# Summing the paths of a grouped convolution two steps of pairs later, with more buffers for the pairs and fewer for the results

## The chip, the cores and the metric

The kernel runs on one core of a Trainium2 chip. The metric is the device time of one execution in microseconds. TensorE (PE) multiplies matrices into PSUM, VectorE (DVE) and ScalarE (ACT) work elementwise and empty PSUM, GpSimd (POOL) does small elementwise work here and issues the indirect DMAs, and SyncE (SP) issues the plain DMAs.

## The reference

The input is `x`, 8 images of 56 x 56 positions with 256 channels. Layer 0 is a block with 32 parallel paths, layer 1 is attention followed by a mixture of experts:

```python
# layer 0: 32 paths, each 256 -> 4 -> (3x3) 4 -> 256 channels
h = relu(bn(einsum('nhwc,cd->nhwd', x, w1) + b1))
h = relu(bn(conv3x3(h, w2) + b2))
h = relu(bn(einsum('nhwd,dc->nhwc', h, w3) + b3))
x = relu(h.sum(over the 32 paths) + x)
# layer 1: t = the positions as tokens, 8 heads of 32 channels
t = t + attention(layernorm(t))   # q (layernorm(k)^T layernorm(v)) / N, plus its input
# 8 experts, each token goes to its two best
t = t + moe(layernorm(t))         # out = tokens + sum of weight * (gelu(tokens w1 + b1) w2 + b2)
```

The ReLU of each path comes before the sum over the paths, so each of 32 x 256 channels must be computed and passed through the ReLU before it can be added.

## The kernel before

**Chunks and slots.** The positions of one image (3136) are cut into 7 chunks of 448; 8 images make 56 chunks. The main loop runs over slots `s`. In slot `s` it computes the last convolution of chunk `s` (`conv3_steps`), the first of chunk `s+2`, the second of chunk `s+1`, the end of chunk `s-1` (`end_steps`: ReLU of the sum, transposes, head means, variances, the products k^T v), the attention and routing of the chunk eight slots back, and a number of tiles of the experts (`moe_steps`), of 256 tokens each. From slot 57 on nothing of the convolution is left: the last attention chunks and the remaining expert tiles form a tail.

**The order.** TensorE, ScalarE and VectorE execute in program order; the program order within a slot is made by `issue`. Each group of work gets a stretch of the slot, such as 0.12 to 1.0 for `end_steps`; each of its steps has a weight and is placed in the middle of its share of the stretch; all steps are sorted by these positions. GpSimd's and SyncE's instructions are ordered by the framework.

**Pairs and sums.** `conv3_steps` has 32 pairs per chunk, two to a step, so 16 steps of pairs. A pair (`pair`) is two products of 64 x 448 into two PSUM tiles (L587), each of which holds four paths of 32 channels. ScalarE writes relu(first + bias) into a buffer `r` (L592), and VectorE adds max(second, -bias) to it in place (L595), which completes the ReLU up to a constant that is added later. Four pairs form a unit, so a chunk has eight units. `sum_paths` (L608) multiplies the four buffers `r` of a unit by `gather`, a matrix of zeros and ones, which adds up the four paths and places the results in four column groups of one PSUM bank. Units 0 to 3 accumulate the first 128 channels, units 4 to 7 the other 128; after the last unit of each half VectorE adds `x` and writes `u` (L615). `begin` in `end_steps` applies the ReLU to `u` on ScalarE (L643), and TensorE transposes it (`tu`, L655).

In the kernel before, unit `u` is summed behind the step that starts with pair 4u+4, which is the step after the unit's last pair. The last unit of a chunk is summed in the next slot, behind its first step.

**Other work on the same engines.** In `end_steps`, VectorE sums the heads (`hmean`, L667), GpSimd centers (`norm`, L681), ScalarE squares (`sq`, L690), VectorE prepares the variances (`hsd`, L718), GpSimd takes their power (L719), and VectorE makes the inverse (`hinv`, L727).

**PSUM.** Products take their tiles from a pool `ps_mm` of seven banks, in a ring; the sums have one bank of their own (`ps_sum`).

**Experts.** A tile of the experts loads rows and weights, transposes the rows (`te`, L1245), multiplies (`ph`, L1287, then `py`, L1303 and L1307), and ScalarE writes the scaled result to a buffer `y` (L1311), two halves per tile. GpSimd adds each half to the output rows with an indirect DMA (L1325). These scatters are ordered in blocks: those of the second choice of a group of chunks wait until those of the first choice have landed, and so on.

Of the kernel before, what the change touches and what calls it, by code (L numbers as in the profile page):

```python
# [8 lines left out]
F32 = mybir.dt.float32  # L9
BF16 = mybir.dt.bfloat16  # L10
I32 = mybir.dt.int32
F32R = mybir.dt.float32r
AF = mybir.ActivationFunctionType
ALU = mybir.AluOpType
# [11 lines left out]
def kernel(  # L26
# [24 lines left out]
    nc = tc.nc  # L51
    B, N, C = x.shape
# [3 lines left out]
    E = w1.shape[0]  # L56
    HC = 32
    NH = C // HC
    P = 128
# [15 lines left out]
    const = ctx.enter_context(tc.tile_pool(name="const", bufs=1))  # L75
# [90 lines left out]
    setup = setup_pool.__enter__()  # L166
# [36 lines left out]
    for dx in range(3):  # L203
        for g in range(NG):
            nc.scalar.dma_start(
                out=W2s[32 * dx : 32 * dx + 32, g],
                in_=W2[32 * g : 32 * g + 32].rearrange(
                    "q (dy dx o) -> dx q dy o", dy=3, dx=3
                )[dx],
# [18 lines left out]
    def is_chunk(s):  # L228
        return 0 <= s < S
# [176 lines left out]
    for f in range(NF):  # L406
        tp = ps_mm.tile([P, 512], F32, tag="mm", name=f"tp_sb_{f}")
        nc.tensor.transpose(tp[:, :NP], bias3[:, f * P : (f + 1) * P], ident[:NP, :NP])
        b3T = setup.tile([P, NP], F32, name=f"b3T_{f}")
        nc.scalar.copy(b3T, tp[:, :NP])  # L410
        sub = setup.tile([P, NQ, NPL], F32, name=f"sub_{f}")
        nc.vector.tensor_copy(
            sub, b3T.rearrange("q (a r n) -> q a r n", r=2, n=NPL)[:, :, 1, :]
        )
        nc.vector.tensor_reduce(
            sumb[:, f, :], sub.rearrange("q a n -> q (a n)"), AX.X, ALU.add
        )
    setup_pool.__exit__(None, None, None)

    spill = ctx.enter_context(  # L420
        tc.tile_pool(name="spill", bufs=NCH + 4, space=bass.MemoryType.DRAM)
    )
    parts = ctx.enter_context(tc.tile_pool(name="parts", bufs=7))
    one = ctx.enter_context(tc.tile_pool(name="one", bufs=1))
    attn = ctx.enter_context(tc.tile_pool(name="attn", bufs=2))
    payp = ctx.enter_context(tc.tile_pool(name="payp", bufs=3))
# [3 lines left out]
    work = ctx.enter_context(tc.tile_pool(name="work", bufs=2))  # L430
# [39 lines left out]
    M = 2 * E + 1  # L470
# [12 lines left out]
        tc.dram_tile([E * CAPR, ROW], F32, name=f"regions_{k}") for k in range(2)  # L483
    ]
    Wd = tc.dram_tile([E, P, WROW], F32, name="Wd")

    b2hl = const.tile([P, C], F32R, name="b2hl")
    b2s = const.tile([P, C], F32, name="b2s")
    b2l = const.tile([E, C], F32R, name="b2l")
    nc.gpsimd.memset(b2s, 0.0)  # L490
    nc.sync.dma_start(out=b2s[:E], in_=b2)
    nc.vector.tensor_copy(b2hl, b2s)
    nc.vector.tensor_tensor(b2l, b2s[:E], b2hl[:E].bitcast(F32), ALU.subtract)
    nc.sync.dma_start(out=b2hl[E : 2 * E].bitcast(F32), in_=b2l.bitcast(F32))
    pos_i = const.tile([P, 2], I32, name="pos_i")
    pos = const.tile([P, 2], F32, name="pos")
    nc.gpsimd.iota(pos_i, [[P, 2]], base=0, channel_multiplier=1)
# [39 lines left out]
    for e in range(M):  # L537
        nc.gpsimd.memset(offs[:, e : e + 1], float(0 if e == 2 * E else e % E * CAPR + TR))
        nc.gpsimd.memset(code[:, e : e + 1], float(E - e % E))

    below = const.tile([P, M, M], F32, name="below")
    nc.gpsimd.memset(below, 1.0)
    nc.gpsimd.affine_select(
        out=below, in_=below, compare_op=ALU.is_ge, fill=0.0, base=-1,
# [8 lines left out]
        out=earlier, in_=earlier, compare_op=ALU.is_ge, fill=0.0, base=-1,  # L553
# [23 lines left out]
    def pair(s, step):  # L577


        cg, ab, c4 = step // 16 * 4 + step % 4, step // 4 % NQ, step % 4  # L580
        hl = h2s[s]
        tiles = [
            ps_mm.tile([P, 512], F32, tag="mm", name=f"c3_{s}_{step}_{g}") for g in range(2)
        ]
        for g in range(2):
            rows = slice(64 * g, 64 * g + 64)
            product = nc.tensor.matmul(  # L587
                tiles[g][:, :CH], W3hl[rows, ab, cg, :], hl[rows, ab, :], start=True, stop=True
            )
        pace[:] = [product.ins]  # L590
        r = parts.tile([P, CH], F32, tag="r", name=f"r_{s}_{step}")
        nc.scalar.activation(  # L592
            r, tiles[0][:, :CH], AF.Relu, bias=b3t[:, cg, 2 * ab : 2 * ab + 1]
        )
        nc.vector.scalar_tensor_tensor(  # L595
            r, tiles[1][:, :CH], nb3[:, cg, 2 * ab + 1 : 2 * ab + 2], r,
            op0=ALU.max, op1=ALU.add,
        )
        unit[s, step] = r

    def sum_paths(s, u):

        f, ab = divmod(u, NQ)
        if ab == 0:
            sums[s, f] = ps_sum.tile([P, 512], F32, tag="su", name=f"su_{s}_{f}")
        ps = sums[s, f]
        for c4 in range(4):
            nc.tensor.matmul(  # L608
                ps[32 * c4 : 32 * c4 + 32, :CH], gather, unit.pop((s, 4 * u + c4)),
                start=(ab == 0), stop=(ab == NQ - 1),  # L610
            )
        if ab == NQ - 1:
            if f == 0:
                usum[s] = one.tile([P, NF, CH], F32, tag="u", name=f"u_{s}")
            nc.vector.scalar_tensor_tensor(  # L615
                usum[s][:, f, :], sums.pop((s, f))[:, :CH], sumb[:, f, :], xTs[s][:, f, :],
                op0=ALU.add, op1=ALU.add,
            )

    def conv3_steps(s):  # L620
        steps = []
        units = NF * NQ
        for step in range(0, 4 * units, 2):
            if is_chunk(s):
                steps.append((0.7, lambda step=step: (pair(s, step), pair(s, step + 1))))
            if step == 0 and is_chunk(s - 1):
                steps.append((0.9, lambda: sum_paths(s - 1, units - 1)))
            if step and step % 4 == 0 and is_chunk(s):
                steps.append((0.9, lambda step=step: sum_paths(s, step // 4 - 1)))
        return steps  # L630

# [561 lines left out]
    got, weights_of, turned, hidden, ready = {}, {}, {}, {}, []  # L1193
# [73 lines left out]
    def bank_of(i, h, name):  # L1267

        if h == 0:
            n = 1 if apart else 2  # L1270
            v = ps_mm.tile([P, n, 256], F32, tag="mm", name=f"{name}_{i}")
            hidden[i, name] = v
        elif apart:
            v = ps_mm.tile([P, 1, 256], F32, tag="mm", name=f"{name}_{i}_{h}")
        else:
            v = hidden[i, name]
        return v[:, h % v.shape[1], :]
# [17 lines left out]
    def tile_out(i, h):  # L1295
        w = weights_of[i]
        eT, g, _ = turned[i]
        if h == 0:
            hidden[i].append(work.tile([P, 2, C], F32, tag="y", name=f"y_{i}", bufs=4))
        hT, y = hidden[i]  # L1300
        own = slot_of[i][1]
        ps = bank_of(i, h, "py")
        nc.tensor.matmul(  # L1303
            ps, own.to_broadcast([P, P]), b2hl, start=True, stop=False
        )
        for f in range(NF):
            nc.tensor.matmul(  # L1307
                ps, hT[:, f, h * P : (h + 1) * P], w[:, (NF + f) * C : (NF + f + 1) * C],
                start=False, stop=(f == NF - 1),
            )  # L1310
        nc.scalar.activation(y[:, h, :], ps, AF.Identity, scale=g[:, h : h + 1])  # L1311
        ready.append((i, h))
# [32 lines left out]
    def moe_steps(first, last):  # L1345


        steps = []

        def some(fn, i, *args):  # L1350
            if 0 <= i < N_ALL:
                fn(i, *args)

        for n in range(first, last):
            steps.append((0.5, lambda n=n: (some(tile_in, n), tile_add())))
            steps.append((1.0, lambda n=n: (some(tile_mid, n - 1, 0), tile_add())))
            steps.append((1.0, lambda n=n: (some(tile_mid, n - 1, 1), some(take_rows, n + 2))))
            steps.append((1.0, lambda n=n: (some(tile_out, n - 2, 0), some(take_weights, n + 1))))
            steps.append((1.0, lambda n=n: some(tile_out, n - 2, 1)))
        return steps  # L1360
# [34 lines left out]
    for s in range(S + A + 1):  # L1395
        a = s - A
        work_of = []
        if s <= S:
            work_of.append((0.0, 1.0 if is_chunk(s) else 0.1, conv3_steps(s)))
# [104 lines left out]
```

## Time and profile before

| | |
|---|---|
| time, median of 3 runs | 3379.75 us (3368.15 to 3382.17) |
| profiled execution | 3374.9 us, granted TensorE clock 0.951 |
| slots 0 to 7, from first pair to first pair | 37.5 to 40.3 us |
| slots 8 to 15 | 42.5 to 60.4 us |
| slots 16 to 54 | 41.6 to 71.1 us, median 51 us |
| last sum of paths | 2820 us |
| tail after it | 555 us |
| `r` on VectorE, L595 | 1792 of 676 ns |
| `r` on ScalarE, L592 | 1792 of 636 ns |
| sums on TensorE, L608 | 3584 records, 574.5 us busy |
| scatter-add issue on GpSimd, L1325 | 420 of 1578 ns |

How to read it: the busy shares of the engines are averages over stages that differ, the main stage with the convolution and the tail with the experts alone, so the stages have to be looked at one by one. TensorE's records show when a product was issued; a product that waits for its operand is issued late, and the others of the same sum lie before it. The time that TensorE stands between two records of one sum is counted neither as idle time before the sum nor as a long record, unless the records no longer touch.

### The profile page before, as it was taken

How to read it: one execution, taken by the hardware profiler on the slowest of the kernel's cores; microseconds unless marked ns; L12 is line 12 of the kernel's file. 1: busy time of each engine (PE TensorE's matmuls, PEld its weight loads, DVE VectorE, ACT ScalarE, POOL GpSimd, SP SyncE). 2: the span in 40 equal slices, each digit the busy share in tenths (PEclk: the TensorE clock that was granted, in tenths of full speed). 3: DMA queues.
4: the chain of work that ended last, by engine and by line, in shares of the span. 5: the costliest groups of instructions: out<-in, count | busy, mean ns of one | idle time of the engine just before them, and what ended most of it. 6: DMA issues, size and time to landing. Idle time of an engine off the chain costs nothing. (4 is left out here: it accounts for less than half of the span.)

```text
span 3374.9 us, 55166 instructions
## 1 busy us (share of the span) xinstructions
PE 3001.6 (89%) x16677; PEld 1697.5 (50%) x16677; DVE 2179.8 (65%) x5762; ACT 1895.8 (56%) x3799; POOL 1928.4 (57%) x1386
## 2 busy tenths in 40 slices
PE   5888888888898999999999999899989987888698
PEld 2343433443444554555545555455444545676577
DVE  3666777777877777776776777776777774333200
ACT  2656555545565666566655666566656654443345
POOL 2222244444556566657565666746656657777677
PEclk7999989989999999999999999999999999988799
DMA  6432334445466676666666667567665756888797
GB/s 146 121 86 84 91 103 123 120 123 150 129 162 159 164 197 168 166 165 174 175 163 163 159 185 187 148 177 187 158 180 152 187 149 159 201 217 218 173 222 178
DMA packets 341481, 537.72 MB, mean 159 GB/s; under 512 B 59952, under 2 KB 251584, under 8 KB 341184
## 3 DMA queue, kind: packets, MB, share of 16 engines
q1 hardware_dynamic: 257088, 429.93, 43.8%
q0 software_dynamic: 81984, 103.45, 16.9%
q8 instruction: 134, 2.20, 0.3%
q14 instruction: 163, 1.34, 0.1%
q10 hardware_dynamic: 2112, 0.81, 0.1%
HBM read 248.01 MB, written 192.55 MB: 131 GB/s over the span
## 5 line engine op out<-in xcount | busy, mean ns | idle before, releaser
L595 DVE SCALAR_TENSOR_TENSOR r<-c,nb,r 128x448 f32<-128x448 f32 x1792 | 1127.3, 676 | 556.7 <-ACT r L592 482.8
L592 ACT ACTIVATE r<-c,b3t 128x448 f32<-128x448 f32 x1792 | 1033.2, 636 | 359.4 <-PE c L587 338.6
L1325 POOL DMA_INDIRECT out_dram<-y,index x420 | 662.8, 1578 | 356.3 <-ACT y L1311 243.7
L587 PE MATMUL c<-hl,W3hl 64*128 64x448 f32 x3584 | 708.4, 428 | 74.4 <-ACT r L592 37.7
L608 PE MATMUL su<-r,gather 128*32 128x448 f32 x3584 | 574.5, 568 | 64.9 <-DVE r L595 38.4
L1031 POOL DMA_INDIRECT regions<-pay,rrowi x448 | 433.1, 967 | 314.1 <-PE c L587 204.2
L587 PEld LDWEIGHTS c<-hl,W3hl 64*128 64x128 f32 x3584 | 341.9, 188 | 505.6 <-issue 227.1
L1287 PE MATMUL ph<-eT,w 128*128 128x256 f32 x1680 | 468.1, 410 | 55.7 <-DMA w<-Wd 23.8
L1307 PE MATMUL py<-w,hT 128*128 128x256 f32 x1680 | 435.6, 384 | 0.0
L1311 ACT ACTIVATE y<-py,g 128x256 f32<-128x256 f32 x420 | 196.7, 475 | 402.1 <-PE py L1307 303.1
L1287 PEld LDWEIGHTS ph<-eT,w 128*128 128x128 f32 x1680 | 306.9, 198 | 196.9 <-issue 101.8
L719 POOL TENSOR_TENSOR hsd<-hsd,half 112x36 f32<-112x36 f32 x56 | 351.7, 6280 | 78.4 <-DVE hsd L718 77.7
L1291 ACT ACTIVATE hT<-ph,w 128x256 f32<-128x256 f32 x420 | 198.1, 477 | 308.5 <-PE ph L1287 165.6
L1307 PEld LDWEIGHTS py<-w,hT 128*128 128x128 f32 x1680 | 293.9, 193 | 28.7
L681 POOL TENSOR_TENSOR norm<-t,hmean 112x512 f32<-112x512 f32 x112 | 120.2, 1130 | 322.1 <-PE c L587 175.0
L870 PE MATMUL at<-tab,tT 128*112 128x272 f32 x896 | 266.1, 421 | 11.9 <-ACT y L1311 6.8
L608 PEld LDWEIGHTS su<-r,gather 128*32 128x32 f32 x3584 | 104.2, 110 | 272.9 <-issue 135.5
L1303 PE MATMUL py<-b2hl,own 128*128 128x256 f32 x420 | 178.7, 425 | 22.4 <-ACT pay L894 8.1
L870 PEld LDWEIGHTS at<-tab,tT 128*112 128x112 f32 x896 | 149.4, 181 | 92.0 <-issue 17.3
L297 PE MATMUL c<-R,W2t 96*32 96x448 f32 x1344 | 180.1, 567 | 3.9 <-DMA R<-h 3.0
L894 ACT ACTIVATE pay<-X,nm,rs 112x256 f32<-112x256 f32 x224 | 134.9, 603 | 75.1 <-DVE nm L889 64.4
L976 POOL TENSOR_TENSOR rq<-ebase,rq 112x8 f32<-112x8 f32 (+1 forms) x32 | 52.9, 1654 | 197.0 <-DVE rq L975 197.0
(246 smaller groups left out, 3198.5 us busy)
## 6 DMA issues: line engine op xcount, KB each, us to landing
w<-Wd SPq DMA_DIRECT2D x210, 513.0 KB
rows<-regions SPq DMA_DIRECT2D x210, 259.0 KB
xi<-in_x_dram SPq DMA_DIRECT2D x56, 448.0 KB
hl<-hi SPq DMA_DIRECT2D x448, 56.0 KB
tTs<-u SPq DMA_DIRECT2D x56, 448.0 KB
ts<-t SPq DMA_DIRECT2D x56, 448.0 KB
tT<-tTs SPq DMA_DIRECT2D x56, 448.0 KB
X<-ts SPq DMA_DIRECT2D x56, 448.0 KB
```

What stands on the lines that cost most here:

```text
L587: product = nc.tensor.matmul(tiles[g][:, :CH], W3hl[rows, ab, cg, :], hl[rows, ab, :], start=True, stop=True)
L592: nc.scalar.activation(r, tiles[0][:, :CH], AF.Relu, bias=b3t[:, cg, 2 * ab : 2 * ab + 1])
L595: nc.vector.scalar_tensor_tensor(r, tiles[1][:, :CH], nb3[:, cg, 2 * ab + 1 : 2 * ab + 2], r, op0=ALU.max, op1=ALU.add,)
L608: nc.tensor.matmul(ps[32 * c4 : 32 * c4 + 32, :CH], gather, unit.pop((s, 4 * u + c4)), start=(ab == 0), stop=(ab == NQ - 1),)
L719: nc.gpsimd.tensor_tensor(sd, sd, half[:T, :].rearrange("q (k h) -> q k h", k=KT), ALU.pow)
L870: nc.tensor.matmul(ps, tT[:, f, k * T : (k + 1) * T], tables_of[b][:, f, :], start=(f == 0), stop=(f == NF - 1),)
L1031: ins = nc.gpsimd.indirect_dma_start(out=regions[n], out_offset=bass.IndirectOffsetOnAxis(ap=v["row_i"][:, (m - group[0]) * KT + k, n : n ...
L1287: nc.tensor.matmul(ps, w[:, f * C + hf * P : f * C + (hf + 1) * P], eT[:, f, :], start=(f == 0), stop=(f == NF - 1),)
L1291: nc.scalar.activation(hT[:, hf, :], ps, AF.Gelu, bias=w[:, 2 * NF * C + hf : 2 * NF * C + hf + 1])
L1307: nc.tensor.matmul(ps, hT[:, f, h * P : (h + 1) * P], w[:, (NF + f) * C : (NF + f + 1) * C], start=False, stop=(f == NF - 1),)
L1311: nc.scalar.activation(y[:, h, :], ps, AF.Identity, scale=g[:, h : h + 1])
L1325: ins = nc.gpsimd.indirect_dma_start(out=out_rows, out_offset=at, in_=y[:, h, :], in_offset=None, compute_op=ALU.add, **partial,).ins
```

## The change

The sum of a unit moves one more step of pairs back: it comes behind the second step after the unit's last pair. The last unit of a chunk is summed behind the second step of the next slot. In between, eight pairs are in hand where it was six, so the pool of buffers `r` grows from seven to nine. Room for them in SBUF comes from three places: the buffers `y` of the experts' results go from four to three; the two helpers that split the experts' second bias into a high and a low part (`b2s`, `b2l`) move from the permanent pool into the setup pool, whose space is reused; and the mask `below`, which has only zeros and ones, becomes bf16. It is for giving TensorE work between a pair and its sum while ScalarE and VectorE finish the pair.

```diff
+    b2hl = const.tile([P, C], F32R, name="b2hl")
+    b2s = setup.tile([P, C], F32, name="b2s")
+    b2l = setup.tile([E, C], F32R, name="b2l")
...
     setup_pool.__exit__(None, None, None)
...
-    parts = ctx.enter_context(tc.tile_pool(name="parts", bufs=7))
+    parts = ctx.enter_context(tc.tile_pool(name="parts", bufs=9))
...
-    b2hl = const.tile([P, C], F32R, name="b2hl")
-    b2s = const.tile([P, C], F32, name="b2s")
-    b2l = const.tile([E, C], F32R, name="b2l")
...
-    below = const.tile([P, M, M], F32, name="below")
+    below = const.tile([P, M, M], BF16, name="below")
...
         for step in range(0, 4 * units, 2):
             if is_chunk(s):
                 steps.append((0.7, lambda step=step: (pair(s, step), pair(s, step + 1))))
-            if step == 0 and is_chunk(s - 1):
+
+            if step == 2 and is_chunk(s - 1):
                 steps.append((0.9, lambda: sum_paths(s - 1, units - 1)))
-            if step and step % 4 == 0 and is_chunk(s):
+            if step > 4 and step % 4 == 2 and is_chunk(s):
                 steps.append((0.9, lambda step=step: sum_paths(s, step // 4 - 1)))
...
-            hidden[i].append(work.tile([P, 2, C], F32, tag="y", name=f"y_{i}", bufs=4))
+            hidden[i].append(work.tile([P, 2, C], F32, tag="y", name=f"y_{i}", bufs=3))
```

## The prediction

> **What bounds the kernel now.** I read the busy table and the slices first, then stretches of time, then the sums by themselves, then single waits.
>
> ```profile
> PE 3001.6 (89%) x16677; PEld 1697.5 (50%) x16677; DVE 2179.8 (65%) x5762; ACT 1895.8 (56%) x3799; POOL 1928.4 (57%) x1386
> ...
> 85.00:388.00 303.00, 259.29 (x1476) 114.87 (x1468) 207.98 (x407) 177.72 (x321) 71.66 (x35) 0.97 0.34 94
> 388.00:750.00 362.00, 305.22 (x1662) 141.85 (x1662) 275.53 (x684) 195.69 (x380) 168.11 (x116) 0.90 0.39 113
> 750.00:2820.00 2070.00, 1941.10 (x11109) 1035.31 (x11108) 1521.45 (x3911) 1270.35 (x2543) 1255.33 (x850) 0.98 0.64 167
> 2820.00:3375.00 555.00, 449.38 (x2258) 381.31 (x2258) 146.40 (x680) 234.31 (x525) 408.01 (x291) 0.91 0.81 199
> ```
>
> TensorE is the busiest engine everywhere, but least so before 750 us (slots 0 to 15, 85% busy against VectorE's 69 to 76%); up to 2820 us it is at 94%; then comes a tail of 555 us with no conv work. The change acts on the sums (L608), which end at 2820 us.
>
> "Busy" hides something there. A sum is eight records, two for each of its four pairs. Undisturbed, their starts lie within 0.42 us. I read all 448 sums record by record: where a later pair's result is missing, TensorE starts the first records and stands still inside the sum. The excess over 0.42 us adds up to 200 us: 112.5 us in the sums of unit 5 of the chunk, 46.6 in unit 2, 9.1, 6.5, 11.2 and 10.6 in units 1, 3, 4 and 7. Slots 0 to 15 hold 112 us of it, slots 16 to 55 88 us. The timeline of one slot shows why unit 5:
>
> ```profile
> 274.76 6.13 POOL L719 TENSOR_TENSOR hsd<-hsd,half 112x36 f32<-112x36 f32 x1 [6.69 <-DVE hsd L718]
> ...
> 278.97 0.94 PE L608 MATMUL su<-r,gather 128*32 128x448 f32 x4
> ...
> 280.92 0.19 DVE L727 SCALAR_TENSOR_TENSOR hinv<-hsd 112x32 f32<-112x32 f32 x1 [2.32 <-POOL hsd L719]
> ...
> 281.46 2.42 DVE L595 SCALAR_TENSOR_TENSOR r<-c,nb,r 128x448 f32<-128x448 f32 x4
> ...
> 282.16 1.53 PE L608 MATMUL su<-r,gather 128*32 128x448 f32 x4 [2.25 <-DVE r L595]
> ```
>
> VectorE stands at `hinv` until GpSimd's power is ready; the four pair results queued behind it come only then, and TensorE stands with half of a sum issued. Over slots 0 to 55 the list of waits has these two entries:
>
> ```profile
> PEld c L587 <- ACT r L592: 152.0, 281, 3.0
> ...
> DVE hinv L727 <- POOL hsd L719: 67.5, 46, 3.2
> ```
>
> The first is the other limit: the pair products wait for a PSUM bank that ScalarE has not yet emptied.
>
> In the tail, GpSimd's rows show the scatters (L1325) 1.85 us apart, in runs of eight with a gap between:
>
> ```profile
> 3215.09 1.54 POOL L1325 DMA_INDIRECT out_dram<-y,index  x1 [0.30 <-issue]
> 3221.91 1.54 POOL L1325 DMA_INDIRECT out_dram<-y,index  x1 [5.28 <-ACT y L1311]
> 3223.76 1.54 POOL L1325 DMA_INDIRECT out_dram<-y,index  x1 [0.30 <-issue]
> ```
>
> The chain that ended last passes, from 3189 to 3249 us, through the landing of such scatters (4.4 to 6.0 us each) into `ACT y`: four `y` buffers are full there.
>
> **What the Trainium skill says.** "Trainium Architecture — The Big Picture", What this means for kernel authors: engines are independent and one blocks another only through a semaphore. The excerpt agrees: GpSimd's power reaches TensorE only over VectorE, so moving a sum behind other work is what can hide it. "Perfetto Trace Analysis", Matmuls: independent matmul groups should rotate through PSUM banks so that one's evacuation overlaps the next's products. The 152.0 us wait shows that seven banks do this incompletely, and it limits the gain below. [...]
>
> **The change part by part.** Let pN be the step with pairs N and N+1, Su the sum of unit u (pairs 4u to 4u+3). A slot's order comes from positions between 0 and 1, worked out from the weights. Before: p20 .644, S4 .6875, hinv .69, p22 .731, p24 .769, S5 .8125, p26 .856, p28 .894. After: p20 .644, p22 .682, hinv .69, S4 .7255, p24 .769, p26 .807, S5 .8505, p28 .894. So every second pair step comes 4.9% of a slot (some 2.5 of 51 us) earlier against all other work, and sums come 3.8% later.
>
> *Unit 5.* p22 now stands ahead of hinv on VectorE, so S5 no longer needs anything behind that wait. The first instruction that does is p28: pair 28's first product takes the bank seven allocations back, the second product of pair 24, whose result is the first behind hinv, where S5 had needed the second. TensorE gains p26 (0.67 us) and half of S5 (0.5 us) as cover, and the needed result is 0.6 us earlier: up to 1.8 us less standing per slot. Capping each slot's measured excess at 1.8 us leaves 14.0 + 13.9 us in slots 0 to 15 and 41.3 us in 16 to 55.
>
> *Units 1, 3, 4, 7.* Their pairs are two steps old at the sum; the excess goes: 27.5 us in slots 0 to 15, 10.1 after.
>
> *Unit 2.* S2 waits for pair 11 behind VectorE's `hmean` (1.21 us). In the new order p14 stands before S2 and needs the banks of pairs 10 and 11, so it waits for the same result. But p14's evictions now come ahead of ScalarE's `sq`, which waits for GpSimd. Ends nothing and all; I take 40%: 10.6 us early, 8.0 later.
>
> *How much passes to the end.* From slot 16 on TensorE is 94% busy, so I pass on 80%: 0.8 x (41.3 + 10.1 + 8.0) = 47.5 us. Before that ScalarE and VectorE take turns with it: 60%, 0.6 x (27.9 + 27.5 + 10.6) = 39.6 us. Gain 87 us.
>
> *Nine buffers of pairs.* Eight pairs are issued when a sum runs, where it was six with seven buffers; the one spare stays. The write of pair 4u+9 waits for Su, which is ahead of that pair's own products on TensorE, so it hides: 0.
>
> *The slot's start.* S7 of the last chunk moves from .0625 to .1005, ScalarE's `u` (L643) stays at .125, and evictions of p4 and TensorE's turn of `u` are queued behind it. Today `u` starts 2.04 us after S7 ends. New order in slot 5: S7 would end about 1.6 us later (255.5 instead of 253.9), VectorE's `u` (0.68 us) then stands behind pairs 2 and 3 and ends near 256.5, where ScalarE started at 255.98 until now: 0.5 us late, with TensorE waiting at `tu` already. From slot 16 on the attention product (1.17 us, L870) and the router's small VectorE work lie there and hide it. 16 x 0.5 = 8 us; ends 0 and 56 x 1.4 = 78, if nothing hides.
>
> *Three `y` buffers.* I took each tile's `y` start and the start of its second scatter; with landings of 4.4 to 6.0 us, a `y` would find its buffer three tiles back unlanded in 33 to 43 of 210 cases, all after 2870 us, and with four in 3 to 11. Between 3182 and 3250 us GpSimd sets the pace (8 x 1.85 + 5.2 = 20 us for four tiles, 5.0 a tile, against 4.13 a tile of TensorE later): a buffer is back 6.0 + 0.5 us after its last scatter, and the tile three on is due at GpSimd after five more scatters, 9.25 us. Hidden. From 3258 us TensorE sets it, and there the counted delays are 1.9 to 3.5 us once, kept to the end: 3 us, with 1 for the earlier ones, 4 us; ends 0 and 12.
>
> *The rest.* The bias split (0.29 and 0.41 us on VectorE at 64 us) only moves ahead in the setup, and `below` as bf16 is read in 17 instructions of 0.28 to 0.75 us: 0, at most 1 us either way.
>
> Sum: 3380 - 87 + 8 + 4 = 3305 us.
>
> **The rivals.**
>
> - *The wait moves to the banks.* The ring of seven makes a later pair wait for nearly the result the sum had waited for. For it: 152.0 us of bank waits, and S2 as worked out. Against: p22 passes hinv. Only pairs handed on earlier remain, some 20 us, against 12 of costs: 3372 us, no change.
> - *Slower: the later sum 7 and the fewer `y`.* ScalarE stands for VectorE's `u` in every slot and half passes on (39 us), the tail costs 12, the gain is 20: 3411 us. For it: ScalarE is in order and two steps of evictions lie behind `u`. Against: it is 56% busy, and after slot 16 other work fills the place.
> - *A larger gain.* Once TensorE runs ahead, the gaps of VectorE go too (it waits 477.8 us for evictions), and all 200 us of standing go with part of TensorE's 74 us of idle before products: 3380 - 200 + 12 = 3192 at the extreme, 3230 as a middle. Against: GpSimd's power and the banks don't get faster.
>
> **How the numbers follow.** Main case 0.62, larger gain 0.13, banks 0.13, slower 0.12. The prediction is the main case, 3305 us. Its pass-on share and unit 2 move it between 3250 and 3350; the range goes on down to 3240, short of half of the larger gain, and up to 3395, which takes in the banks and part of the slower case. Faster by over 0.5%: 0.62 + 0.13 + a third of the banks' case, 0.79; within: 0.09; slower: 0.12.
>
> **What would show it.** Right: the starts inside S5 lie within 0.42 us in nearly all slots, `hinv` still waits for GpSimd, slots before 750 us get 2 to 3 us shorter and later ones about 1 us, and the tail is some 4 us longer with more `ACT y` waits on scatters. Wrong: TensorE's waits before products (L587) grow by what the sums lose; or ScalarE's `u` waits over a microsecond for VectorE in late slots too; or the tail grows by more than 12 us.

## The result, and the profile after

The changed kernel takes 3495.95 us (median of 4 runs, 3484.67 to 3501.05), the kernel before 3376.24 us in the same runs: 1.0352 times as long, 95% interval 1.0314 to 1.0389. The forecast of 3305 us was wrong in direction, and the time lies outside its range of 3240 to 3395 us.

First the busy table and the same four stretches as before: their bounds, length, then busy time (with instructions) of PE, PEld, DVE, ACT and POOL, granted clock, DMA share and GB/s.

```profile
PE 3044.4 (87%) x16677; PEld 1742.9 (50%) x16677; DVE 2170.5 (62%) x5762; ACT 1906.8 (55%) x3799; POOL 1922.0 (55%) x1386
...
85.00:388.00 303.00, 256.39 (x1422) 110.81 (x1422) 201.62 (x389) 174.03 (x308) 71.64 (x35) 0.91 0.30 87
388.00:758.00 370.00, 310.46 (x1700) 146.53 (x1696) 276.38 (x696) 199.07 (x386) 166.88 (x116) 0.88 0.39 114
758.00:2928.00 2170.00, 1978.33 (x11118) 1078.17 (x11114) 1513.27 (x3909) 1280.03 (x2547) 1247.33 (x850) 0.95 0.61 159
2928.00:3490.00 562.00, 455.91 (x2281) 385.25 (x2279) 149.58 (x686) 236.09 (x528) 410.64 (x293) 0.90 0.80 197
```

From first pair to first pair, slots 0 to 15 take 700.8 us (685.4 before), slots 16 to 55 take 2169.9 (2071.9), the tail 561.8 (557.7). So of the 115 us between the two profiled executions, 98 were lost where the forecast saw a gain of 47. VectorE, ScalarE and GpSimd are busy for the same time as before within 0.6%; what is longer is time in which something waits, and in the third stretch the clock fell from 0.98 to 0.95.

The groups of instructions on TensorE (busy us, mean ns, then idle us before them with the releasers); from the loop of `conv3_steps` on, a line of the changed kernel has a number one higher than before:

```profile
L587 PE MATMUL c<-hl,W3hl 64*128 64x448 f32 x3584 | 780.1, 440 | 134.9 <-ACT r L592 59.2 <-DVE r L595 50.3 <-DMA hl<-lo 9.2
L608 PE MATMUL su<-r,gather 128*32 128x448 f32 x3584 | 448.5, 571 | 4.3 <-DVE u L615 4.3
L748 PE MATMUL kv<-norm 112*128 112x129 f32 x896 | 173.2, 358 | 79.2 <-POOL norm L738 78.8 <-DVE r L595 0.2
L656 PE MATMUL tu<-ident,u 128*112 128x128 f32 x448 | 73.5, 289 | 39.3 <-ACT u L644 39.2
```

The sums did what the change is for: the standing inside them (what the starts of a sum's eight records exceed 0.42 us by, added over all 448 sums) fell from 200.0 to 11.2 us, their busy time from 574.5 to 448.5, the idle time before them from 64.9 to 4.3. But idle time before the products k^T v (`kv`, L747 before) grew from 16.9 to 79.2 us, before the pair products from 74.4 to 134.9, and before `tu` from 18.6 to 39.3. TensorE's records name the releaser, GpSimd's `norm` at L738, which the forecast had not looked at. The list of waits shows the same chain, engine by engine (us in total, times, longest):

```profile
PEld c L587 <- ACT r L592: 231.7, 454, 5.2
POOL hsd L720 <- DVE hsd L719: 146.5, 46, 10.9
DVE kvs L756 <- PE kv L748: 119.4, 47, 8.1
DVE hinv L728 <- POOL hsd L720: 100.2, 49, 7.8
PE kv L748 <- POOL norm L738: 78.8, 73, 4.0
ACT y L1312 <- DMA out_dram<-y,index: 60.7, 19, 10.0
ACT u L644 <- DVE u L615: 50.0, 31, 2.5
PE tu L656 <- ACT u L644: 39.2, 31, 1.8
```

Before, GpSimd's power waited 77.7 us for `hsd`, `kvs` 17.8 for `kv`, `hinv` 75.3, `kv` 1.2 for `norm`, `tu` 8.1 for `u`. The timeline of one slot of the changed kernel shows where the lateness begins; it is put together from the lines of VectorE, GpSimd and TensorE. ScalarE has finished the squares of this chunk at 1575.37 us:

```profile
1576.54 1.28 DVE L595 SCALAR_TENSOR_TENSOR r<-c,nb,r 128x448 f32<-128x448 f32 x2 [2.28 <-ACT r L592]
...
1580.06 1.28 DVE L595 SCALAR_TENSOR_TENSOR r<-c,nb,r 128x448 f32<-128x448 f32 x2 [0.98 <-ACT r L592]
1581.25 1.21 DVE L700 TENSOR_REDUCE hss<-sq 112x32 f32<-112x1024 f32 x1
...
1583.57 0.17 DVE L719 TENSOR_SCALAR hsd<-hss 112x32 f32<-112x32 f32 x1
...
1583.83 6.16 POOL L720 TENSOR_TENSOR hsd<-hsd,half 112x36 f32<-112x36 f32 x1 [2.43 <-DVE hsd L719]
...
1590.02 0.19 DVE L728 SCALAR_TENSOR_TENSOR hinv<-hsd 112x32 f32<-112x32 f32 x1 [2.03 <-POOL hsd L720]
...
1592.86 0.68 PE L587 MATMUL c<-hl,W3hl 64*128 64x448 f32 x4
...
1594.43 2.61 POOL L738 TENSOR_TENSOR norm<-norm,hinv 112x512 f32<-112x512 f32 x2
...
1596.09 0.49 PE L748 MATMUL kv<-norm 112*128 112x129 f32 x2 [2.55 <-POOL norm L738]
1597.09 3.38 PE L748 MATMUL kv<-norm 112*128 112x129 f32 x14 [0.52 <-POOL norm L738]
```

Read it downwards: the first instruction of the variances (`hss`) could have run at 1575.4, but VectorE is in order, and ahead of `hss` stand four pair results that wait for ScalarE: counted through, those at 1576.54 are of pairs 16 and 17, those at 1580.06 of pairs 18 and 19. It starts 5.9 us after its input. This slot is a mild case: over slots 16 to 54 the mean of this distance is 7.9 us, before the change 5.5. Then everything is in series: `hsd`, GpSimd's power of 6.16 us, `hinv`, GpSimd's scaling, and only then the products, for which TensorE has been standing 2.55 us.

Over slots 16 to 54 (the ends of chunks 15 to 53), in us from the slot's first pair, the means were:

| | before | after |
|---|---|---|
| S7 ends | 3.62 | 5.04 |
| last `t` (copy of the transposes) ends | 12.58 | 13.29 |
| `sq` starts | 23.23 | 24.48 |
| `hss` starts | 29.87 | 33.54 |
| GpSimd's power ends | 39.12 | 42.38 |
| `kv` ends | 48.63 | 50.82 |
| slot ends | 51.94 | 54.40 |

S7 is the last sum of a chunk. From `sq` to `hss` it takes 6.64 us before and 9.06 after: 2.4 us are added just there, and 1.25 us have come in earlier. With S7 alone put back (an experiment below) `sq` starts at 23.40 us again, so most of the 1.25 us is S7's.

The slot's order explains the 2.4 us. Position of the variances: 0.56, in both kernels. The step p18 (pairs 18 and 19) is at 0.606 before and at 0.557 after. It slid past the variances, by 0.003 of a slot, and VectorE's program order in the changed kernel has the results of pairs 18 and 19 ahead of `hss` instead of behind it.

### The profile page after: what moved, and what is told of

The parts are those of the page before. It is cut to its first block, busy times and chain, and to the rows that moved or that the text cites. A ratio compares the mean times of both kernels' runs of the same rounds, so it can differ in the third digit from the quotient of the medians.

```text
span 3489.8 us, 54857 instructions
## 1 busy us (share of the span) xinstructions
PE 3044.4 (87%) x16677; PEld 1742.9 (50%) x16677; DVE 2170.5 (62%) x5762; ACT 1906.8 (55%) x3799; POOL 1922.0 (55%) x1386
## 5 line engine op out<-in xcount | busy, mean ns | idle before, releaser
L587 PE MATMUL c<-hl,W3hl 64*128 64x448 f32 x3584 | 780.1, 440 | 134.9 <-ACT r L592 59.2
L587 PEld LDWEIGHTS c<-hl,W3hl 64*128 64x128 f32 x3584 | 363.0, 192 | 588.1 <-ACT r L592 231.7
L608 PE MATMUL su<-r,gather 128*32 128x448 f32 x3584 | 448.5, 571 | 4.3 <-DVE u L615 4.3
L875 DVE SCALAR_TENSOR_TENSOR X<-at,rs,X 112x256 f32<-112x256 f32 x224 | 107.3, 479 | 230.8 <-PE at L871 230.7
L748 PE MATMUL kv<-norm 112*128 112x129 f32 x896 | 173.2, 358 | 79.2 <-POOL norm L738 78.8
L748 PEld LDWEIGHTS kv<-norm 112*128 112x128 f32 x896 | 150.6, 256 | 106.0 <-POOL norm L738 100.2
```

The source lines that it names most:

```text
L587: product = nc.tensor.matmul(tiles[g][:, :CH], W3hl[rows, ab, cg, :], hl[rows, ab, :], start=True, stop=True)
L608: nc.tensor.matmul(ps[32 * c4 : 32 * c4 + 32, :CH], gather, unit.pop((s, 4 * u + c4)), start=(ab == 0), stop=(ab == NQ - 1),)
L748: nc.tensor.matmul(ps[:, f, :], norm[:, k, mine], norm[:, k, f * P : f * P + P + 1], start=(k == 0), stop=(k == KT - 1),)
```

## The experiments

The theory: p18 ahead of the variances is the main loss, the late S7 the second. The rivals: the nine buffers, the three `y` and what was moved for them; the later sums themselves, through the ring of banks; the lower clock.

**Only the buffers.** The kernel before, with everything of the diff but the two conditions that place the sums.

> The changed kernel with the order of pairs and sums of the kernel before: only the nine r buffers, the three y buffers, the moved bias split and the bf16 mask are left. Theory C (buffers): about 3496 us. A, B and D: 3376 to 3386 us, some 4 us of it in the tail from the third y buffer.

Measured: 3393.57 us, 1.0028 times before (1.0016 to 1.004). The buffers are not the cause of 3.5%, but the 0.3%, some 9 us (5 to 14 by the interval), is more than the 4 us that the forecast gave to the three `y`, the nine buffers and the rest together. Two more runs take it apart. With four `y` again (`bufs=3` back to `bufs=4`):

> The order of the kernel before with nine r buffers, the moved bias split, the bf16 mask and four y buffers, so that against the run with the buffers alone only y differs. If the 9 us which that run lost come from y: 3376 to 3386 us, ratio 0.999 to 1.001. If they come from the rest: ratio 1.002 or more.

Measured: 3397.64 us, 1.0032 (1.0018 to 1.0047). So the loss is not that of the three `y`. And with seven `r` again as well (`parts`, `bufs=9` back to `bufs=7`), so that only the moved bias split and the bf16 mask are left:

> The kernel before with only the bias split moved into the setup pool and the mask in bf16; seven buffers of pairs and four of results as before. The kernel before with nine buffers of pairs beside these two took 1.0032 times as long [1.0018, 1.0047]. If the two extra buffers of pairs cost that (through other moments at which writes may start), this kernel takes as long as before, 0.9985 to 1.0015. If the moved split or the mask cost it (other addresses, another type in the router's products), it takes 1.002 to 1.005 times as long.

Measured: 3386.1 us against 3377.54, 1.0025 (1.0014 to 1.0036). So the nine buffers of pairs cost nothing that shows, and the split or the mask, or what else moves in SBUF with them, costs 8 us. Which of them was not tried; one profile of each kernel has most of the difference between slots 8 and 24 (slot 24 begins 1093.6 us after the first pair, 1079.2 before), far behind the split itself.

**The variances first.** In the changed kernel, the group `end_steps` begins at 0.11 of the slot, which moves its steps by at most 0.01 and puts the variances at 0.555, ahead of p18:

```diff
-            work_of.append((0.12, 1.0, end_steps(s - 1)))
+            work_of.append((0.11, 1.0, end_steps(s - 1)))
```

> The changed kernel with the end of a chunk placed from 0.11 of the slot instead of 0.12, so that the variances (0.555) stand ahead of the pairs 18 and 19 (0.557) again. Theory A (the pairs 18 and 19 put themselves ahead of the variances on VectorE, the chain from there over GpSimd's power to the products kv starts 2.5 to 3.7 us later in each slot, and TensorE stands at kv and loses its clock): the loss of about 116 us goes, 3330 to 3390 us, kv waits for GpSimd under 20 us. Theory B (the later last sum delays u and the whole end of the chunk), C (the buffers) and D (the ring of banks): stays at 3480 to 3500 us.

Measured: 3386.8 us, 1.0012 times before (0.9997 to 1.0027). Of the 119 us lost, this gives 115 back (1.0352 less 1.0012, of 3380). The 0.01 also changes two other orders in some slots: the transposes `tu` and the squares come ahead of a step of the experts. That is the smaller part, since on average `sq` starts 0.31 us earlier than in the changed kernel and `hss` 2.38 us. The timeline of the same chunk in this kernel, in which the squares end at 1509.85:

```profile
1515.02 1.21 DVE L700 TENSOR_REDUCE hss<-sq 112x32 f32<-112x1024 f32 x1
1517.33 0.18 DVE L719 TENSOR_SCALAR hsd<-hss 112x32 f32<-112x32 f32 x1
1517.41 1.27 DVE L595 SCALAR_TENSOR_TENSOR r<-c,nb,r 128x448 f32<-128x448 f32 x2
...
1517.60 6.16 POOL L720 TENSOR_TENSOR hsd<-hsd,half 112x36 f32<-112x36 f32 x1 [0.17 <-DVE hsd L719]
...
1523.92 0.18 DVE L728 SCALAR_TENSOR_TENSOR hinv<-hsd 112x32 f32<-112x32 f32 x1
...
1528.21 2.64 POOL L738 TENSOR_TENSOR norm<-norm,hinv 112x512 f32<-112x512 f32 x2
...
1529.89 0.49 PE L748 MATMUL kv<-norm 112*128 112x129 f32 x2 [0.34 <-POOL norm L738]
```

The pair results at 1517.41 now stand behind `hsd`, the power runs beside them, `hinv` no longer waits, and TensorE stands 0.34 us at `kv`. In this chunk `hss` starts 5.2 us after its input, only 0.7 us sooner than in the changed kernel; over slots 16 to 54 it starts at 31.16 us on average (33.54 in the changed kernel), 5.8 us after its input (7.9). The list of waits:

```profile
POOL hsd L720 <- DVE hsd L719: 57.5, 29, 7.3
PE tu L656 <- ACT u L644: 39.7, 33, 1.8
PE kv L748 <- POOL norm L738: 38.0, 51, 3.1
DVE hinv L728 <- POOL hsd L720: 31.8, 25, 7.8
```

The waits of the chain halve or better, though `kv` still waits 38.0 us for GpSimd where under 20 had been expected. The wait of `tu` stays: S7 is still late.

**A like order put into the kernel before.** The variances moved behind p18, without anything of the change:

```diff
-            (1.0, center), (0.6, squares), (1.8, variances), (0.8, inverse), (0.8, scale),
+            (1.0, center), (0.6, squares), (0.5, lambda: None), (1.8, variances), (0.3, inverse), (0.8, scale),
```

> The kernel before with one edit: an empty step of weight 0.5 ahead of the variances, taken from the inverse behind them, so that the variances stand behind the pairs 18 and 19 as in the changed kernel, with everything else in place. Theory A: the loss appears without the change, 3420 to 3500 us, and kv waits for GpSimd. B, C and D: 3370 to 3385 us.

Measured: 3645.19 us, 1.0756 (1.0716 to 1.0797), 256 us and far more than in the changed kernel or than expected. (`hinv` moves from 0.69 to 0.715 with it, still between the same steps of pairs.) Its waits and its sums show where it goes:

```profile
DVE hinv L727 <- POOL hsd L719: 235.5, 56, 7.6
PE su L608 <- DVE r L595: 232.2, 55, 5.9
...
DVE u L615 <- PE su L608: 50.2, 51, 3.5
...
L608 PE MATMUL su<-r,gather 128*32 128x448 f32 x3584 | 619.7, 596 | 232.2 <-DVE r L595 232.2
```

In the order of before, S5 still needs pair results from behind `hinv`, so lateness of the power stands in the sum as well (393.2 us of standing, 311.5 of them in unit 5). And the order is not quite that of the changed kernel: at 0.61 the variances are also behind S3 (0.5625), so VectorE's `u` of the first half stands ahead of `hss` too, and waits 50.2 us for TensorE (8.6 in the kernel before). `hss` starts 9.9 us after its input, not 7.9. So this run shows that the place of the variances alone can cost more than the change did; it is no measure of what p18 alone costs.

**S7 back in its place.** The changed kernel with the first of its two conditions undone:

```diff
-            if step == 2 and is_chunk(s - 1):
+            if step == 0 and is_chunk(s - 1):
```

> The changed kernel with only the last sum of a chunk back behind the first step of the next slot; the variances stay behind the pairs 18 and 19. Theory A (variances): the loss stays, 3450 to 3500 us. Theory B (the late last sum holds up u, its transposes and the chunk's end): 3400 us or less.

Measured: 3445.16 us, 1.017 (1.0124 to 1.0216), between what the two theories had expected. The waits of the slot's start go, those of the chain stay: `tu` waits 8.2 us for `u` (39.2 in the changed kernel), `kv` 78.3 us for `norm` (78.8). And with the variances first too:

> Both at once: the variances ahead of the pairs 18 and 19 and the last sum early, all other sums two steps late. If the late last sum is what kept the run with the variances first at 3387 us: 3340 to 3365 us, slots before 750 us as short as there and later ones no longer than before the change. If it costs nothing: 3380 to 3392 us.

Measured: 3332.41 us, 0.9849 (0.9799 to 0.9899), faster than the kernel before. The four together, as ratios to before:

| | variances behind p18 | variances first |
|---|---|---|
| S7 behind the second step | 1.0352 (the change) | 1.0012 |
| S7 behind the first step | 1.017 | 0.9849 |

Of 3380 us, the variances are worth 115 or 109 us, S7 62 or 55: the two nearly add, and without both what is left of the change saves 51 us. In the groups of TensorE of this last kernel

```profile
L587 PE MATMUL c<-hl,W3hl 64*128 64x448 f32 x3584 | 755.1, 432 | 129.0 <-ACT r L592 50.1 <-DVE r L595 49.3 <-DMA hl<-lo 10.7
L608 PE MATMUL su<-r,gather 128*32 128x448 f32 x3584 | 447.1, 569 | 0.0
L748 PE MATMUL kv<-norm 112*128 112x129 f32 x896 | 140.9, 310 | 45.3 <-POOL norm L738 40.8 <-ACT r L592 3.6
```

the sums wait for nothing, but the idle time before the pair products is almost that of the changed kernel (134.9). So the wait for banks and pair results comes with later sums (139.3 us in the next kernel, whose pairs stay in place), and does not by itself make the kernel slower.

**Later sums with the pairs in place.** An empty step keeps every pair and `end_steps` where they were before; units 0 to 6 are summed one step later, S7 as before:

```diff
-            if step == 2 and is_chunk(s - 1):
+            if step == 0 and is_chunk(s - 1):
                 steps.append((0.9, lambda: sum_paths(s - 1, units - 1)))
+            if step and step % 4 == 0 and is_chunk(s):
+                steps.append((0.9, lambda: None))
             if step > 4 and step % 4 == 2 and is_chunk(s):
-                steps.append((0.9, lambda step=step: sum_paths(s, step // 4 - 1)))
+                steps.append((0.0, lambda step=step: sum_paths(s, step // 4 - 1)))
```

> The changed kernel with the pairs at the places of the kernel before (an empty step keeps the gap) and the last sum of a chunk behind the first step of the next slot as before; units 0 to 6 are still summed one step later. Theory A: the variances stand ahead of the pairs 18 and 19, so no loss: 3330 to 3385 us, and the standing inside the sums is still gone in part. Theory D (a later sum makes later pairs wait for banks, whatever else): 3440 us or more. Theory B: 3376 or less, since the last sum is early.

Measured: 3361.9 us, 0.9927 (0.9899 to 0.9955). Later sums are a gain when nothing else moves, though a smaller one than with the pairs moved up and the variances ahead of them.

**The clock.** In the changed kernel TensorE runs at half clock for 511 us from the first pair on, before for 294. "TensorE: Matmul & The Clock Gate" in the Trainium skill, under Part 1: The HAM clock gate (the "warmup" mystery), says that the array has two clocks, full and half, set by how busy it has been over windows of some 3.4 us. The records agree: in the whole execution 38 stretches at half clock take 3.41 us, 38 take 6.83 and 6 take 10.24, and four of the other five are longer multiples of 3.41. To see how much of the loss is the clock's own, six products of the identity with itself stand ahead of `kv` in its bank, so that TensorE works where it stood. They are added work and are overwritten:

```diff
+            for n in range(6):
+                nc.tensor.matmul(ps[:, 0, :P], ident, ident, start=True, stop=True)
             for f in range(NF):
```

> The changed kernel with six extra products of the identity with itself written into the tile of kv just ahead of its own products, which overwrite them: they fill part of the time in which TensorE stands there, and cost up to 6 x 0.22 x 56 = 74 us where it doesn't stand. If the lower clock is a loss of its own, brought on by the standing: the time at half clock falls from 511 to under 430 us and the kernel gets faster than 3480 us. If the waits are all there is: half clock unchanged or nearly, 3496 to 3560 us.

Measured: 3482.92 us, 1.0289 (1.024 to 1.0338), an interval that overlaps that of the change: half clock went as the first theory expected, the time as neither did. The groups of TensorE:

```profile
L750 PE MATMUL kv<-norm 112*128 112x129 f32 x896 | 133.9, 305 | 26.0 <-POOL norm L738 25.5
L746 PE MATMUL kv<-ident 128*128 128x128 f32 x672 | 104.6, 314 | 6.5 <-DVE r L595 5.3
```

Most of the standing at `kv` is filled (32.5 us of idle time before both lines, 79.2 without the added products) and half clock falls from 511 to 400 us, yet the time hardly moves. That is not clean, since the added products take 104.6 us of their own. Beside it stands the kernel with the pairs in place, which has 444 us at half clock and is faster than before. So half clock doesn't decide the time alone; its own share of the loss stays open.

**The variances earlier still.** If p18 ahead of the variances costs, having them further ahead might gain. In the kernel before, at 0.50 in place of 0.56 (the 0.494 of the expectation is the next kernel's place), one more step of pairs earlier:

```diff
-            (1.0, center), (0.6, squares), (1.8, variances), (0.8, inverse), (0.8, scale),
+            (1.0, center), (0.6, squares), (0.6, variances), (1.2, lambda: None), (0.8, inverse), (0.8, scale),
```

> The kernel before with the variances at 0.494 instead of 0.56 of the slot, ahead of the pairs 16 and 17 (the weight taken from them goes to an empty step behind). Theory A says that the chain from the variances over GpSimd's power to the inverse sets what VectorE and TensorE wait for, also before the change: the inverse waits less for the power, the sums of unit 5 stand less, 3290 to 3350 us. If VectorE then waits for the squares instead: 3376 us or slower.

Measured: 3398.03 us, 1.0037 (1.0022 to 1.0053): no gain, where 3290 to 3350 us had been expected. `hinv` hardly waits for the power now (5.1 us, 75.3 before) and unit 5 stands 83.3 us instead of 112.5, as expected, but the time moves elsewhere:

```profile
DVE nm L889 <- POOL rs L885: 232.6, 55, 25.3
```

The power of 6.2 us on GpSimd now comes ahead of the router's small `rs`, and VectorE stands for that one (92.7 us in the kernel before). The same edit on the best kernel below:

> The kernel with the variances first, the last sum early and four y buffers, with the variances moved on to 0.494 of the slot, ahead of the pairs 16 to 19. If the chain behind the variances still sets the slot: 3290 to 3315 us. If, as in the kernel before with this edit, GpSimd's power now stands ahead of the attention's own power: 3335 us or slower.

Measured: 3372.35 us, 0.996 (0.9944 to 0.9975), against 0.9823 without it, with `nm` waiting 232.9 us for `rs`. So the variances can also come too early.

**The best of them.** Variances first, S7 early, and four buffers `y` as in the kernel before:

> The kernel with the variances first and the last sum early, with four y buffers instead of three (nine r buffers stay). Theory C in the small (the third y buffer's loss is in the tail): 3 to 10 us faster than the same kernel with three, 3322 to 3330 us, and a tail of 556 to 558 us instead of 559.4. If the fourth buffer does nothing: 3332 us, within 2.

Measured: 3327.34 us, 0.9823 (0.9796 to 0.9849). It beats both kernels. Against three `y` (3332.41) the intervals overlap; the waits of `ACT y` on scatters fall from 62.9 to 36.1 us, the tail from 559.4 to 557.5. This kernel also holds nine `r` and four `y` at once, so with the moved split and the bf16 mask the change had room for the fourth `y`.

## Why the prediction was wrong

*The standing in the sums* (*Unit 5*, *Units 1, 3, 4, 7*, *Unit 2*): right in kind, too small in size. The text took 125 of the 200 us away; 189 went. Of 112.5 us in unit 5 1.2 are left, where the cap of 1.8 us a slot had left 43; of 46.6 in unit 2, where only 40% had been taken, 3.7; of 37.4 in units 1, 3, 4 and 7 2.9. `hinv` still waits for GpSimd, as it said. But not all that left the sums was covered: the idle time before the pair products grew by 60 us.

*The slot's order*: this is the step that failed. The text worked out that "every second pair step comes 4.9% of a slot" earlier against all other work, and then followed it at a few places only: p22 with hinv, p14 with `sq`, and the slot's start. It did not go through the other instructions that a pair step could pass, and so put the cost of all the others at nothing. p18 passed the variances by 0.003 of a slot, and they head a chain in series: two visits to GpSimd before TensorE may go on. The cost is 109 to 115 us, shown by taking it out of the changed kernel with S7 in either place. The run that put a like order into the kernel before shows the direction alone. The forecast's argument for p22 is the same one with the sign turned: a pair step moved ahead of a wait helps those who need the pairs, a pair step moved ahead of the start of a chain delays the chain.

*The slot's start*: this failed too, in size and not in mechanism. 8 us were costed (16 x 0.5); S7's place is worth 55 to 62, about 1 us in each of 56 slots. What failed is the claim that from slot 16 on the attention product and the router's work hide it. In slots 16 to 55 the idle time before `tu` went from 8.8 to 22.5 us, more than in slots 0 to 15 (9.2 to 16.0), and with S7 back it went again. How the remainder of the 55 to 62 us comes about was not followed. The end of 78 held it.

*How much passes to the end*: near early, partly by luck, and wrong late. The kernel with the variances first and S7 early ("mended" in the table) tells it. The table takes the time from each TensorE record's start to the next one's and counts it for the group that comes next; the last row but one is all that began at half clock, and the others hold the rest.

| us | slots 0-15: before | mended | slots 16-55: before | after | mended |
|---|---|---|---|---|---|
| sums, L608 | 180.7 | 91.3 | 296.1 | 223.1 | 220.9 |
| pairs, L587 | 205.4 | 237.4 | 479.7 | 518.0 | 517.0 |
| `kv` | 23.8 | 45.6 | 93.8 | 122.9 | 109.9 |
| all other | 180.1 | 180.7 | 1116.4 | 1080.9 | 1104.2 |
| at half clock | 95.4 | 83.5 | 86.3 | 225.1 | 116.4 |
| sum | 685.4 | 638.5 | 2072.3 | 2170.0 | 2068.4 |

In slots 0 to 15, 89 us leave the sums and 47 reach the end, 53%. The forecast's 39.6 us came near it with 60% of too small a gain, 66 us. In slots 16 to 55, 75 us leave the sums and 12 all other work; 37 come back at the pairs, 16 at `kv`, and 30 more are at half clock: 4 us, less than two executions of a kernel differ by, reach the end where 47.5 had been forecast. That TensorE is 94% busy there was taken as a sign that it sets the pace. The table shows freed time turning into waits one step on, before the pairs and `kv`; that the evictions and the chain over GpSimd set the pace in turn with TensorE is how it reads, and no run takes these apart. To that extent the rival of the banks was right for the late slots; as a whole it fell, since it gave 3372 us with nothing lost elsewhere.

*Nine buffers of pairs*: right, 0. *Three `y` buffers*: within its ends of 0 and 12 us; the tail grew by 4.1 us in the changed kernel, and taking the fourth back gave 5 us, which the intervals don't separate from none. *The rest*: 0, "at most 1 us either way", was too little; the moved split and the mask cost 8 us (5 to 12 by the interval), by a way that stays open.

In sum: the later sums and what moved with them saved 51 us, the 8 us of split and mask and the cost of the three `y` already taken off, where 83 had been forecast (87 less 4), the late S7 cost 55 for 8, and the variances 115 for nothing. -51 + 55 + 115 = 119 us, the 3.5% measured; it is one way through the table of four kernels. The rival that ended on the slower side had the late S7 at 39 us, nearer than the main case, but at 3411 us it missed the variances as well.

Two of the signs of being wrong did come, one of them in part: the waits of TensorE before L587 grew by 60 us, a third of what the sums lost in standing, and ScalarE's `u` waited for VectorE in late slots too (45.1 us in 28 places after 758 us). The mended kernel has the first sign too and is faster, so it didn't tell right from wrong.

## What to carry to other kernels

Where a schedule is made by sorting positions, an edit that adds, removes or moves one step moves all of its group: write out the new order of every in-order engine and look at each pair of instructions that changed places, above all at what now stands ahead of the first instruction of a chain that visits other engines. A distance of 0.003 of a slot cost more here than the change was meant to gain. And TensorE's busy share of 94% didn't mean here that time freed on it reaches the end: look for what the engine would wait for next.

## What the hardware showed

- Standing that is spread differently gave a different clock. In slots 16 to 55 the changed kernel has 46 stretches at half clock, the kernel before 19, although the 88 us of standing inside the sums there had gone. What had grown were gaps ahead of `kv`, `tu` and the pairs: of 2 us or more there were 28 for 15, and only 2 of the 28 (1 of the 15) were as long as a window of 3.41 us. In the 3.41 us ahead of each of the 46 stretches the longest gap was 0.77 to 2.88 us, so a gap needn't fill a window to come with half clock. Nor does the count of such gaps tell: the kernel with the pairs in place has 12 of them and 33 stretches.
- Moving a setup step and narrowing a mask together, neither of which has a visible cost in its own records, changed the time by 0.25% (1.0014 to 1.0036, 22 runs against 27); why stays open.
